# Two-layer graph network: the blocks of the adjacency matrix that are checked for symmetry are transposed by DMA instead of by TensorE

## The chip, the cores and the metric

The kernel runs on one core of a Trainium2 chip. A core has TensorE for matrix products (PE in the profile, its weight loads PEld), VectorE (DVE), ScalarE (ACT), GpSimd (POOL) and SyncE (SP), which here only issues DMAs. Each engine works through its own queue in order, and semaphores tie the queues together. The metric is the time of one execution on the device, in microseconds; lower is better. The kernel before takes 1238.69 us, the median of three runs from 1237.64 to 1240.6.

## What is computed

Sixteen graphs of 1024 nodes with 128 features go through two layers. The first is masked attention in which a node attends to its neighbours; the second is three GraphSAGE convolutions with batch normalisation over an adjacency that has been thinned row by row ("dilated"). Cut to what matters:

```python
# x: (16, 1024, 128); adj: (16, 1024, 1024) of 0 and 1, symmetric, with ones on the diagonal
h = maximum(layernorm(x), 0)
q, k, v = (relu(h @ W.T + b) for W, b in ((Wq, bq), (Wk, bk), (Wv, bv)))
att = softmax((q @ k.T) * adj - 9e15 * (1 - adj))
x = x + relu(att @ v @ Wo.T + bo)

h = maximum(layernorm(x), 0)
def step(carry, n):                      # over the rows n, in order
    row = carry[n]
    num = sum(row)
    sf = where(num > 10, (num + 1) // 2, 1)
    rm = row & (cumsum(row) % sf == 0) if num > 1 else 0
    carry[n] &= ~rm; carry[:, n] &= ~rm
adj_d = scan(step, adj > 0)
for Wr, Wx, b, g, be in three convolutions:
    out = (adj_d @ h / deg) @ Wr + h @ Wx + b
    h = bn(relu(out / norm(out)), g, be)
x = x + concatenate([h1, h2, h3]) @ Wl + bl
```

## The kernel before

The kernel has a fast path for inputs of this shape and a general one for all others. The fast path keeps checks of the input beside its work (`verdict`, line 449): zeros and ones only, diagonal full, adjacency symmetric, and some sizes. If a check fails, the general path runs afterwards. The check for symmetry is what the change touches.

**The attention loop.** One step per batch, 16 steps. A step has 2 x 8 scores: TensorE multiplies a block of 128 keys with 512 queries (line 697), ScalarE takes the exponential (line 699), VectorE multiplies it with the adjacency (line 700), and half a step later TensorE multiplies the result with the values (line 713). The step is cut into 48 ticks (`TICKS`), three to a score. `pace` (line 811) runs once a tick: it emits what was put off to this tick (`clock`), and then advances every generator of an agenda that has this tick in its list. The lists (`AT_PROJECT`, `AT_LOAD`, `AT_BOUND`, `AT_MIRRORS`, `AT_SORT`, `AT_GATHER`, `AT_NORMS`, `AT_STORE`, lines 735 to 750) are written out by hand. So the order of the instructions in each engine's queue is the order of the ticks, and no scheduler changes it. Most lists differ for even and odd steps. In step 0 the lists are squeezed into the second half of the step.

**The adjacency.** During step i the rows of batch i+1 are loaded (`load`, line 158): eight times a DMA of 512 KB by SyncE into one of three staging tiles `st`, then a pass of ScalarE that writes the bf16 tile `ab` and sums the rows, and a second pass that counts zeros (`AT_LOAD`: every third tick from tick 1, two ticks to a row block). `ab` has two buffers.

**The check for symmetry.** `mirrors` (line 214) has nine parts at the ticks of `AT_MIRRORS`: the first counts the diagonal (`count_loops`, line 208, which writes a throw-away tile `junkv`), the other eight are `mirror(b, k)` (line 180). For row block k TensorE transposes the k+1 blocks of the column up to the diagonal into a PSUM tile (line 186, 1 to 8 transposes, 36 a batch), and one tick later VectorE compares this tile with `ab`'s row, two bf16 at a time as int32, and sums what differs into `odd` (line 192). The PSUM tile comes from a pool of two (`bank`, line 152) that the other parts of the dilation use too.

**The rest of the dilation.** `bound` (line 221) decides step by step which nodes are "special"; its eight small products wait for `d_away` from VectorE. In odd steps `sort` and `gather` (lines 239 and 284) follow for two batches. `gather` has 13 parts: four that make `onehot`, one product, the rows' index with an indirect DMA of GpSimd (`rows`, line 301), a scan by VectorE (line 305), the codes (line 308), eight transposes by TensorE (line 312), two evictions (line 316), a product (line 320), and the codes' store. `AT_GATHER` has the ticks of these 13 parts, for the even batch within the step and the tick after it, for the odd batch in the next step. `solve` (line 330) then iterates over groups of four batches.

**Where the layers meet.** After step 15 there are 22 more ticks with the last values (line 882). What is left of the agenda then, parts of the last gather alone, goes with the last `solve` into a generator `last_of_dilation` (line 899). It is advanced beside the first convolution by `beside1` (line 1073), eight times a batch, so that `PIECES1` parts are spread evenly over `TICKS1` = 120 of its ticks.

The queues that matter: SyncE issues the adjacency loads, the loads of `x`, and later loads and stores, in program order; GpSimd issues the indirect DMAs, that is the gathers' rows and the scatter of each batch's result (line 540).

Of the kernel before, what the change touches and what calls it, by code (L numbers as in the profile page):

```python
# [8 lines left out]
BF = mybir.dt.bfloat16  # L9
H16 = mybir.dt.float16  # L10
I32 = mybir.dt.int32
AF = mybir.ActivationFunctionType
OP = mybir.AluOpType
AX = mybir.AxisListType

P = 128
B, N, D = 16, 1024, 128
NB = N // P
# [18 lines left out]
LAST = 12  # L37
# [18 lines left out]
class Clock:  # L56


    def __init__(self):
        self.now, self.queue = 0, []  # L60
# [20 lines left out]
class Dilation:  # L81
# [7 lines left out]
    def __init__(self, tc, adj, accT, ones, jp, identf, pool, psum, rows, rows_psum, clock):  # L89

        self.nc, self.adj = tc.nc, adj
        nc = self.nc
        self.accT, self.ones = accT, ones
        self.pick = {}
        self.pool, self.psum, self.rows, self.rows_psum, self.put_off = pool, psum, rows, rows_psum, clock.later
        own = self.pool

        def const(name, shape, dtype=F32):
            return own.tile(shape, dtype, name=name, bufs=1)

        self.identf = identf
        self.identb, self.identh = (const(f"d_id{i}", [P, P], t) for i, t in enumerate((BF, H16)))
        for t in (self.identb, self.identh):
            nc.vector.tensor_scalar(t, jp, 0.0, None, op0=OP.is_equal)
        self.up = const("d_up", [P, P], BF)
        nc.vector.tensor_scalar(self.up, jp, 0.0, None, op0=OP.is_gt)
        self.after = const("d_after", [P, P], BF)
        nc.vector.tensor_scalar(self.after, jp, 0.0, None, op0=OP.is_lt)
        nc.vector.scalar_tensor_tensor(self.after, self.identb, BIG, self.after, op0=OP.mult, op1=OP.add)
        self.onesb = const("d_ones", [P, P], BF)  # L110
        nc.vector.memset(self.onesb, 1.0)
        self.onesf = const("d_onesf", [P, P])
        nc.vector.memset(self.onesf, 1.0)
        self.half = const("d_half", [P, 1], BF)
        nc.vector.memset(self.half, 0.5)
        self.one_k = const("d_one_k", [P, 1])
        nc.vector.memset(self.one_k, -ONE_K)
        ii = const("d_ii", [P, S], I32)
        nc.gpsimd.iota(ii, pattern=[[1, S]], base=1, channel_multiplier=0)
        self.iota = const("d_iota", [P, S], H16)  # L120
        nc.vector.tensor_copy(self.iota, ii)
        mi = const("d_mi", [P, NB], I32)
        nc.gpsimd.iota(mi, pattern=[[P, NB]], base=0, channel_multiplier=1)
        self.node = const("d_node", [P, NB])
        nc.vector.tensor_copy(self.node, mi)
        self.node32 = mi
        self.node16 = const("d_node16", [P, NB], H16)
        nc.vector.tensor_copy(self.node16, mi)
        self.first = [const(f"d_first{i}", [P, NB, 2], BF) for i in range(2)]
        self.away = [const(f"d_away{i}", [P, 2, NB, 3], BF) for i in range(2)]  # L130
        self.limits = [const(f"d_limits{i}", [P, NB, 2]) for i in range(2)]
        self.neghalf = const("d_neghalf", [P, 1], BF)
        nc.vector.memset(self.neghalf, -0.5)
        for t in self.away + self.first:
            nc.vector.memset(t, 1.0)

        self.deg = const("d_deg", [P, B, NB])
        self.zeros = const("d_zeros", [P, B, NB])
        self.odd = const("d_odd", [P, B, NB])
        self.loops = const("d_loops", [P, B])  # L140
        self.sizes = const("d_sizes", [P, B, 2])
        self.used = const("d_used", [P, B])
        self.code = const("d_code", [P, B, S], H16)
        self.own = const("d_own", [P, B, P], BF)
        self.dcode = const("d_dcode", [P, B])
        self.moved = const("d_moved", [P, B])
        self.kept_deg = const("d_kdeg", [P, B])
        self.slot = const("slot", [P, B, NB], I32)
        self.A = {}
        self.tail = False  # L150

    def bank(self, shape, dtype, own=False):
# [5 lines left out]
    def load(self, b):  # L158
# [5 lines left out]
        for k in range(NB):  # L164
# [12 lines left out]
                nc.scalar.activation(junk, st, AF.Exp, scale=-ZERO_K, accum_out=zeros)  # L177
            yield

    def mirror(self, b, k):  # L180

        nc = self.nc
        ab, diag = self.A[b]
        pt = self.bank([P, NB, P], BF)
        for j in range(k + 1):
            nc.tensor.transpose(pt[:, j, :], ab[:, j, k * P:(k + 1) * P], self.identb)
        n = (k + 1) * P // 2

        def compare():

            junk = self.rows.tile([P, NB, P], BF, name="junkv", bufs=1)
            nc.vector.scalar_tensor_tensor(junk.rearrange("p a b -> p (a b)")[:, :n],
                                           pt.rearrange("p a b -> p (a b)").bitcast(I32)[:, :n], 1.0,
                                           ab[:, k, :].bitcast(I32)[:, :n], op0=OP.mult, op1=OP.not_equal,
                                           accum_out=self.odd[:, b, k:k + 1])

        self.put_off(1, compare)

    def prepare(self, b):

# [6 lines left out]

    def count_loops(self, b):
        nc = self.nc
        junk = self.rows.tile([P, NB, P], BF, name="junkv", bufs=1)  # L210
        nc.vector.scalar_tensor_tensor(junk, self.A[b][1], 1.0, self.identb[:, None, :].to_broadcast([P, NB, P]),
                                       op0=OP.mult, op1=OP.mult, accum_out=self.loops[:, b:b + 1])

# [299 lines left out]
def fast(ctx: ExitStack, tc: tile.TileContext, a, out, vp):  # L513
    nc = tc.nc
# [119 lines left out]
    late = ExitStack()  # L634
# [6 lines left out]
    with ExitStack() as s1:  # L641
        att = s1.enter_context(tc.tile_pool(name="att", bufs=2))
        aps = s1.enter_context(tc.tile_pool(name="aps", bufs=2, space=PSUM))
        dil = Dilation(tc, adj, accT, kept, jp, identf, dpool, dpsum,
                       rows.enter_context(tc.tile_pool(name="adj", bufs=2, side="right")), aps, clock)
# [79 lines left out]
        def store(b):  # L725
            for k in range(NB):
# [10 lines left out]
                      for m in ([1, 9, 14, 15, 16], [0, 1, 3, 5, 6])]  # L737
        AT_LOAD = every(1, 2 * NB, 3)
        AT_BOUND = [[0] + [first + 3 * (j // 2) + j % 2 for j in range(2 * NB)] for first in (9, 3)]
        AT_MIRRORS = ([11, 20, 23, 29, 33, 35, 39, 42, 44], [11, 13, 16, 19, 22, 25, 29, 33, 41])  # L740

        AT_SORT = [27, 29, 31, 32, 33, 35, 36]
        AT_GATHER = ([37, 38, 39, 41, 44, 45, 51, 55, 59, 60, 61, 65, 66],
                     [68, 69, 70, 71, 74, 75, 81, 85, 89, 90, 91, 93, 94])
        AT_NORMS = ([30, 57, 67, 68, 71], [42, 44, 58, 67, 70])
        AT_STORE = every(75, NB, 2)
# [2 lines left out]
        agenda = []  # L749
        gathering = {}  # L750

        def plan(gen, start, ticks):
            agenda.append((gen, [start + t for t in ticks]))

        def solve_pieces(b0, b1):
            return 9 * ITER + 3 + 13 * (b1 - b0)

        def plan_step(i):

            start, odd = i * TICKS, i % 2  # L760
            if i == 0:

                late = lambda ticks: [TICKS // 2 + t // 2 for t in ticks]
                plan(values0, start, [3, 6, 9, 12])
            else:
                late = lambda ticks: ticks
            plan(dil.bound(i), start, late(AT_BOUND[odd]))
            plan(dil.mirrors(i), start, late(AT_MIRRORS[odd]))
            if i + 1 < B:
                plan(project(i + 1), start, late(AT_PROJECT[odd]))  # L770
                plan(load_adj(i + 1), start, late(AT_LOAD))
            if odd:
                plan(dil.sort(i - 1), start, AT_SORT)
                for b, ticks in zip((i - 1, i), AT_GATHER):
                    gathering[b] = dil.gather(b)
                    plan(gathering[b], start, ticks)
            if i:
                last = i == B - 1
                plan(norms_of_x2(i - 1, att), start, LAST_NORMS if last else AT_NORMS[odd])
                plan(store(i - 1), start, LAST_STORE if last else AT_STORE)  # L780
            for b0, b1, t0, t1 in GROUPS:
                if t0 // TICKS == i:
                    n = solve_pieces(b0, b1)
                    plan(dil.solve(b0, b1), 0, [t0 + j * (t1 - t0) // n for j in range(n)])
# [3 lines left out]
        def load_adj(b):  # L788
            g = dil.load(b)
            next(g)  # L790
            AB_[b] = dil.A[b][0]
            yield
            yield from g
# [15 lines left out]
        tick = 0  # L809
# [75 lines left out]
        for t in range(22):  # L885
# [3 lines left out]
            b = t // 4 - 1  # L889
# [2 lines left out]
                    H[b] = enter(b)  # L892
                _advance(H[b][1])
        clock.flush()
        assert all(gen is gathering[B - 1] for gen, ticks in agenda if ticks)
        dil.tail = True
    load_x2(2)

    def last_of_dilation():

        yield from gathering[B - 1]
        yield from dil.solve(LAST, B)

    def last_stores():
# [158 lines left out]
    with tc.tile_pool(name="ps1", bufs=2, space=PSUM, reuse_waits="tile") as ps:  # L1063
# [3 lines left out]
        checks = dil.verdict(a["nodemask"], vp, recips)  # L1067
        _advance(checks)

        tick, TICKS1, PIECES1 = 0, 8 * (B - 1), 13 + solve_pieces(LAST, B)  # L1070
        entering = iter(())

        def beside1():
# [782 lines left out]
```

## Time and profile before

| | |
|---|---|
| median of three runs | 1238.69 us |
| the profiled execution | 1234.29 us |
| its span, first to last instruction | 1232.4 us |
| TensorE busy in the span | 1095.0 us (89%), 7775 products |
| VectorE, ScalarE, GpSimd busy | 881.5, 726.6, 573.6 us |
| mean granted TensorE clock | 0.96 |
| line 186, the transposes of adjacency blocks | 576 |
| line 192, their compares | 128 |
| adjacency loads (512 KB each), median to landing | 128, 3.7 us |
| row gathers, median to landing | 16, 4.9 us |

The attention loop takes up about the first 770 us, the first convolution runs to about 920, the other two and the output fill the rest. A line of the timeline or of a group names the line of the code, the engine, the operation and the tiles (written tile, arrow, read tiles), then shapes. In square brackets stands how long the engine had been idle, and what ended that wait. The engines' queues overlap the end of one instruction with the start of the next, so that durations in a row add up to more than the time they take; the distance of starts shows that.

The waits of SyncE's own queue are few and long in the attention loop: it has 8 adjacency loads and one load of `x` to issue in a step of some 46 us.

### The profile page before, as it was taken

To read this page: it belongs to the slowest core of one execution; us is meant where nothing else is said; L and a number is where in the kernel's file an instruction comes from. 1 tells how busy PE (TensorE), PEld (TensorE's weight loads), DVE (VectorE), ACT (ScalarE), POOL (GpSimd) and SP (SyncE) were. 2 spreads that over 40 slices of the span, in tenths; PEclk is the share of its full clock that TensorE was granted. 3 is DMA by queue.
4 is the path that set the end of the run, shared out by engine and by line. 5 is a ranking of instruction groups with operands and counts; after the bars stand their busy time and mean duration, and the time that the engine had idled before them with its cause. 6 is when DMAs were issued, how large, how long until landed. Compare 5 with 4: busy or idle time off the path is not lost. (4 is left out here: it accounts for less than half of the span.)

```text
span 1232.4 us, 22348 instructions
## 1 busy us (share of the span) xinstructions
PE 1095.0 (89%) x7775; PEld 820.4 (67%) x7775; DVE 881.5 (72%) x2630; ACT 726.6 (59%) x1570; POOL 573.6 (47%) x1082
## 2 busy tenths in 40 slices
PE   4899999999899899899899888588769979999894
PEld 2467677666576676566567656477658758988773
DVE  5767567579788578678778778589877876666642
ACT  5578788777677777678677652266554542333320
POOL 0330752651742742743644524769400004777686
PEclk9899999999999999999999999789889989999897
DMA  6544244344244344244334411415000013778564
GB/s 197 157 132 139 92 139 152 99 130 150 87 137 144 98 137 153 86 126 151 97 127 122 125 31 39 122 42 135 1 1 1 1 35 109 228 218 239 167 185 126
DMA packets 118147, 143.45 MB, mean 116 GB/s; under 512 B 9212, under 2 KB 94088, under 8 KB 118024
## 3 DMA queue, kind: packets, MB, share of 16 engines
q1 hardware_dynamic: 106120, 110.78, 30.3%
q0 software_dynamic: 11904, 31.15, 7.7%
q8 instruction: 63, 1.03, 0.4%
q14 instruction: 60, 0.49, 0.1%
HBM read 113.39 MB, written 28.51 MB: 115 GB/s over the span
## 5 line engine op out<-in xcount | busy, mean ns | idle before, releaser
L713 PEld LDWEIGHTS po<-vw,e 128*128 128x128 f32 x2048 | 273.1, 195 | 65.7 <-issue 65.3
L713 PE MATMUL po<-vw,e 128*128 128x129 f32 x2048 | 306.9, 284 | 0.0
L697 PE MATMUL ps<-qT,kT 128*128 128x512 f32 x512 | 272.0, 615 | 0.8 <-ACT e L699 0.8
L700 DVE TENSOR_TENSOR e<-e,ab 128x512 f32<-128x512 f32 x256 | 177.9, 696 | 110.4 <-ACT e L699 108.8
L699 ACT ACTIVATE e<-ps 128x512 f32<-128x512 f32 x256 | 153.0, 598 | 107.1 <-PE ps L697 84.4
L540 POOL DMA_INDIRECT x_d<-xt,slot x128 | 142.6, 1114 | 38.8 <-issue 34.9
L167 ACT ACTIVATE ab<-st,d_one_k 128x1024 bf16<-128x1024 f32 x128 | 146.9, 1148 | 0.3 <-DMA st<-in_adj_dram 0.3
L576 POOL TENSOR_SCALAR ln_t<-ln_st 128x8 f32<-128x8 f32 x31 | 8.0, 258 | 288.5 <-DVE ln_st L569 230.0
L177 ACT ACTIVATE junk<-st 128x1024 bf16<-128x1024 f32 x112 | 118.3, 1056 | 0.0
L540 POOL DMA_INDIRECT y_d<-y,nodes x88 | 86.2, 979 | 29.1 <-issue 28.6
L722 ACT ACTIVATE o<-po,recips 128x128 f32<-128x128 f32 x128 | 46.7, 367 | 72.1 <-DVE recips L720 72.0
L697 PEld LDWEIGHTS ps<-qT,kT 128*128 128x128 f32 x512 | 79.0, 194 | 7.6 <-issue 3.1
L1019 ACT ACTIVATE r<-pt 128x512 f32<-128x512 f32 x74 | 44.5, 601 | 58.7 <-PE pt L1007 58.7
L588 POOL TENSOR_SCALAR hn<-xt,ln 128x128 f32<-128x128 f32 x120 | 75.9, 644 | 1.6
L965 ACT ACTIVATE sq<-po 128x512 f32<-128x512 f32 x80 | 47.7, 596 | 47.1 <-PE po L956 44.1
L951 PE MATMUL po<-ws,r 128*128 128x128 f32 x512 | 74.8, 292 | 0.0
L305 DVE TENSOR_TENSOR_SCAN left<-rows 128x1024 f16<-128x1024 f32 x16 | 38.2, 2389 | 50.1 <-DMA rows<-in_adj_dram,row 50.1
L1016 DVE BATCH_NORM_STATS2 stats<-r 128x6 f32<-128x512 f32 x74 | 50.9, 689 | 29.4 <-ACT r L1019 28.9
L951 PEld LDWEIGHTS po<-ws,r 128*128 128x128 f32 x512 | 64.9, 199 | 8.6 <-issue 6.8
L968 DVE TENSOR_REDUCE nrm<-sq 128x4 f32<-128x512 f32 x80 | 53.9, 676 | 22.8 <-ACT sq L965 21.4
L1149 POOL COPY mark<-y 128x1 f32<-128x1 f32 x30 | 5.7, 191 | 135.7 <-DVE y L1024 132.8
L588 POOL TENSOR_SCALAR hn<-xt 128x128 f32<-128x128 f32 x112 | 55.9, 510 | 27.0 <-PE pt L598 26.2
(300 smaller groups left out, 2426.8 us busy)
## 6 DMA issues: line engine op xcount, KB each, us to landing
st<-in_adj_dram SPq DMA_DIRECT2D x128, 512.0 KB, 3.7
r<-y_d SPq DMA_DIRECT2D x22, 512.0 KB, 5.2
xt<-x_d SPq DMA_DIRECT2D x16, 524.0 KB, 3.8
xt<-in_x_dram SPq DMA_DIRECT2D x16, 512.0 KB, 4.2
x<-x_d SPq DMA_DIRECT2D x16, 512.0 KB, 4.4
out_dram<-r SPq DMA_DIRECT2D x11, 512.0 KB, 3.4
x_d<-xt,slot POOLq DMA_INDIRECT x128, 2.8
y_d<-y,nodes POOLq DMA_INDIRECT x88, 3.5
```

The source lines that it names most:

```text
L167: nc.scalar.activation(ab[:, k, :], st, AF.Exp, bias=self.one_k, scale=ONE_K, accum_out=self.deg[:, b, k:k + 1])
L177: nc.scalar.activation(junk, st, AF.Exp, scale=-ZERO_K, accum_out=zeros)
L540: d = nc.gpsimd.indirect_dma_start(out=dst, out_offset=bass.IndirectOffsetOnAxis(ap=slots, axis=0), in_=src, in_offset=None)
L588: engine.tensor_scalar(hn[:, k, :], xt[:, k, :D], minus[:, k // 2, k % 2, None], rstd[:, k // 2, k % 2, None], op0=OP.add, op1=OP.mult)
L697: nc.tensor.matmul(p, K[b][:, k * P:(k + 1) * P], Q[b][:, c], start=True, stop=True)
L699: later(1, lambda: nc.scalar.activation(e, p, AF.Exp))
L700: later(2, lambda: nc.vector.tensor_mul(e, e, AB_[b][:, k, c]))
L713: nc.tensor.matmul(po[:, q % 2, :], E[k][:, i * P:(i + 1) * P], V[b][:, k, :], start=(k == 0), stop=(k == NB - 1))
L951: nc.tensor.matmul(po[:, i, :], hT[:, c:c + P], wxk, start=(i == 3), stop=False)
L965: later(1, lambda: nc.scalar.activation(sq, halves[g], AF.Square))
L968: nc.vector.tensor_reduce(n[:, 0, 4 * g:4 * g + 4], sq, axis=AX.X, op=OP.add)
L1016: nc.vector.bn_stats(stats[:, 2 * b + g, :], d)
```

## The change

The transposes of the check go from TensorE to DMAs, which SyncE issues. A new generator `turn_rows` takes, for k from 0 to 7, the first (k+1) x 128 columns of `ab`'s row block k and writes its blocks, each transposed, into a tile of its own in SBUF (`mirrored0` to `mirrored7`, one buffer each). `mirror` then is the compare alone: it takes the next of these tiles, compares it with the column of blocks in `ab` that it should equal, and writes the result of the compare over the tile. Before, the column was transposed and compared with the row.

The generator is advanced at the ticks of a new list, `AT_TURN`, the same in all steps: 12 to 15 and 20 to 23 (in step 0 squeezed like the others). At these ticks its DMAs fall between the adjacency loads in SyncE's queue: two each behind the loads that are counted 1 and 2 from 0, four behind load 3. `count_loops` writes into `mirrored7` now. The compares are emitted at the tick at which they were put off to before (the tick of `AT_MIRRORS` and one more).

Two smaller edits go with it. In even steps' gathers the transposes of the codes and their two evictions come two ticks later (61, 62, 63). And in `last_of_dilation` empty parts are put between the parts of the last gather: six behind the part that issues the rows' DMA, five behind the codes. Eleven parts of this gather are left there, and `PIECES1` now counts them as they are, with the empty ones: 11 + 11 + the solver's 118, where before it was 13 + 118.

```diff
+    def turn_rows(self, b):
+        ab = self.A[b][0]
+        for k in range(NB):
+            pt = self.rows.tile([P, k + 1, P], BF, name=f"mirrored{k}", bufs=1)
+            self.nc.sync.dma_start(pt, ab[:, k, :(k + 1) * P], transpose=True)
+            self.mirrored.append(pt)
+            yield
+
     def mirror(self, b, k):
-        nc = self.nc
-        ab, diag = self.A[b]
-        pt = self.bank([P, NB, P], BF)
-        for j in range(k + 1):
-            nc.tensor.transpose(pt[:, j, :], ab[:, j, k * P:(k + 1) * P], self.identb)
-        n = (k + 1) * P // 2
-        def compare():
-            junk = self.rows.tile([P, NB, P], BF, name="junkv", bufs=1)
-            nc.vector.scalar_tensor_tensor(junk.rearrange("p a b -> p (a b)")[:, :n],
-                                           pt.rearrange("p a b -> p (a b)").bitcast(I32)[:, :n], 1.0,
-                                           ab[:, k, :].bitcast(I32)[:, :n], op0=OP.mult, op1=OP.not_equal,
-                                           accum_out=self.odd[:, b, k:k + 1])
-        self.put_off(1, compare)
+        pt = self.mirrored.pop(0)
+        self.nc.vector.scalar_tensor_tensor(pt.bitcast(I32), pt.bitcast(I32), 1.0,
+                                            self.A[b][0][:, :k + 1, k * P:(k + 1) * P].bitcast(I32), op0=OP.mult,
+                                            op1=OP.not_equal, accum_out=self.odd[:, b, k:k + 1])
...
-        junk = self.rows.tile([P, NB, P], BF, name="junkv", bufs=1)
+        junk = self.rows.tile([P, NB, P], BF, name="mirrored7", bufs=1)
...
+        AT_TURN = [12, 13, 14, 15, 20, 21, 22, 23]
...
-        AT_GATHER = ([37, 38, 39, 41, 44, 45, 51, 55, 59, 60, 61, 65, 66],
+        AT_GATHER = ([37, 38, 39, 41, 44, 45, 51, 55, 61, 62, 63, 65, 66],
...
-            plan(dil.mirrors(i), start, late(AT_MIRRORS[odd]))
+            plan(dil.turn_rows(i), start, late(AT_TURN))
+            plan(dil.mirrors(i), start, late([t + (j > 0) for j, t in enumerate(AT_MIRRORS[odd])]))
...
-        assert all(gen is gathering[B - 1] for gen, ticks in agenda if ticks)
+        (gather_left,) = (len(ticks) for gen, ticks in agenda if ticks)
...
+    GATHER_IDLE = {5: 6, 7: 5}
     def last_of_dilation():
-        yield from gathering[B - 1]
+        for part in range(13 - gather_left, 13):
+            next(gathering[B - 1])
+            for _ in range(1 + GATHER_IDLE.get(part, 0)):
+                yield
         yield from dil.solve(LAST, B)
...
-        tick, TICKS1, PIECES1 = 0, 8 * (B - 1), 13 + solve_pieces(LAST, B)
+        tick, TICKS1, PIECES1 = 0, 8 * (B - 1), gather_left + sum(GATHER_IDLE.values()) + solve_pieces(LAST, B)
```

More of the change, by code (lines that the diff above doesn't have):

```diff
@@ L149, in __init__ @@
         self.A = {}
+        self.mirrored = []
         self.tail = False
```

## The prediction

> **What bounds the kernel now.** I read first the busy time of the engines in each step of the attention loop (a step is one of the 16 batches; I cut the windows where VectorE forms `du`, the first instruction of a step), because all removed work lies there. The columns are the window, its length, then busy time and count of TensorE, its weight loads, VectorE, ScalarE, GpSimd, then clock, DMA share and rate.
>
> ```profile
> 69.90:113.10 43.20, 43.20 (x303) 31.06 (x303) 27.66 (x97) 34.52 (x65) 10.67 (x23) 1.00 0.41 112
> ...
> 248.70:295.10 46.40, 45.82 (x343) 32.89 (x342) 38.29 (x142) 35.78 (x70) 24.45 (x45) 1.00 0.42 128
> 295.10:345.10 50.00, 42.23 (x318) 29.43 (x318) 39.80 (x137) 34.11 (x68) 23.45 (x45) 1.00 0.38 122
> ...
> 69.90:770.00 700.10, 653.78 (x4673) 462.23 (x4673) 526.12 (x1788) 502.25 (x975) 327.50 (x631) 0.99 0.38 116
> ```
>
> The reader is to see that TensorE is busy for 653.8 of 700.1 us over steps 1 to 15, VectorE for 526 and ScalarE for 502. In odd steps TensorE hardly pauses (0.0 us in step 1, 0.6 in step 5); in even ones it does (7.8 us in step 6). Second, the timeline of TensorE around one row of adjacency blocks: start, duration, instruction, count.
>
> ```profile
> 339.58 0.61 PE L713 MATMUL po<-vw,e 128*128 128x129 f32 x4
> 340.03 0.61 PE L186 MATMUL pd<-d_id,ab 128*128 128x128 bf16 x8
> 340.47 1.08 PE L697 MATMUL ps<-qT,kT 128*128 128x512 f32 x2
> ```
>
> The durations overlap; the starts don't. Eight transposes hold TensorE from 340.03 to 340.47, 0.055 us each. Third, the waits of steps 1 to 14 (us in total, times, longest), and the timeline where the last gather's tail meets the next layer:
>
> ```profile
> PE pd L233 <- DVE d_away L236: 7.4, 11, 1.4
> ...
> PE pd L312 <- DVE codes L308: 7.0, 7, 1.8
> ```
> ```profile
> 794.01 1.07 POOL L301 DMA_INDIRECT rows<-in_adj_dram,row  x1 [0.16 <-issue]
> ...
> 799.12 3.80 DVE L305 TENSOR_TENSOR_SCAN left<-rows 128x1024 f16<-128x1024 f32 x1 [8.70 <-DMA rows<-in_adj_dram,row]
> 802.95 1.28 DVE L308 SCALAR_TENSOR_TENSOR codes<-rows,left 128x1024 f16<-128x1024 f32 x1
> ...
> 804.29 1.04 PE L312 MATMUL pb<-d_id,codes 128*128 128x128 f16 x8 [12.05 <-DVE codes L308]
> ```
>
> TensorE stands still for 12.05 us in one place, because VectorE stands 8.70 us behind rows that had not landed. Last, what SyncE does, since the new transfers are issued there, and what VectorE's compare costs:
>
> ```profile
> SPq L166 <- ACT junk L177: 355.4, 80, 8.1
> ```
> ```profile
> q1 hardware_dynamic: 106120, 110.78, 30.3%
> ...
> st<-in_adj_dram SPq DMA_DIRECT2D x128, 512.0 KB, 3.7
> ```
> ```profile
> L700 DVE TENSOR_TENSOR e<-e,ab 128x512 f32<-128x512 f32 x256 | 177.9, 696 | 110.4 <-ACT e L699 108.8
> ...
> L192 DVE SCALAR_TENSOR_TENSOR junkv<-pd,ab 128x512 bf16<-128x512 int32 x16 | 11.0, 688 | 5.9 <-PE pd L186 5.9
> ```
>
> SyncE mostly waits for ScalarE to free a staging tile, 4.4 us each time; the DMA engines carry 30% from its queue.
>
> **What the Trainium skill says.** "VectorE: DVE Perf Modes", section "The three transpose paths", gives a 128x128 bf16 transpose 390 ns on TensorE and 1309 ns through the DMA crossbar. For TensorE the trace says 219 ns for one and 55 ns in a row, and the latter is what counts here. "Advanced Engine Details and Errata", section "X-Bar Transpose (TRN2)", calls such DMAs as fast as plain ones, 350 to 400 GB/s. The two disagree by an order of magnitude once transposes follow each other: the blocks of a step are 36 x 32 KB = 1.18 MB, an estimate of 3 us by the second page and, added up, of 36 x 1.309 = 47 us by the first. No run so far shows a DMA transpose. "DMA: Bandwidth & Descriptors", section "Rules for kernel authors", says that DMAs of all queues share the same 16 engines, and that a transpose beside ordinary DMAs needs no ordering. The trace shows those engines 38% busy in steps 1 to 15.
>
> **TensorE loses 576 transposes.** 36 a step x 0.055 = 1.98 us a step, 31.7 us in all. What of it counts depends on whether TensorE sets the pace there. In the seven odd steps from 1 to 13 its idle time is together 3.4 us: I count 95%, 7 x 1.98 x 0.95 = 13.2 us. The seven even steps from 2 to 14 have 38.1 us of idle time, waits for VectorE's bursts, for GpSimd's `hn` and for solver results; a transpose ahead of such a wait only makes the wait longer. Most transposes of an even step lie in its second half (30 of 36 from tick 29 on) and most of those waits in its first: I count 70%, 9.7 us. Step 15 (4.8 us idle) half, 1.0; step 0, where TensorE is busy 25.2 of the 30 us from 40 to 70, 60%, 1.2. Sum 25.1 us; with every wait growing it is some 14, with none 31.7.
>
> **VectorE's compare reads the block from SBUF.** The nearest row is L700, 512 f32 elements from SBUF in 696 ns, against 688 for 512 int32 from PSUM; the eight compares keep their lengths. Cost nothing, between -2 and +2 us of VectorE's time, hidden as long as VectorE is 75% busy. VectorE's 14.8 us of waiting for those transposes goes too, and nothing hung on it. If a block were late, VectorE would stand at the compare, behind it the products for the next values and so TensorE; but the last block is issued at about tick 12 and compared at tick 42 or later, some 28 us.
>
> **SyncE issues 128 transposes, eight a step, between the adjacency loads.** Counting a batch's loads from 0, they stand behind load 1 (two), load 2 (two) and load 3 (four), and loads 4 to 7 of the next batch stand behind them. In step 5 load 3 can go when ScalarE frees its tile at about 254.0; the four transposes behind it hold 26 of the 36 blocks. The eighth waits for the loop count that VectorE ends at 261.2 (both write one tile); load 4 had been due at 259.7, so it goes some 1.5 us late. It is needed by ScalarE at 272.3 and takes 3.7 to land: it may leave at 268.6. So these 26 blocks have 14.6 us, or 0.56 us each, before anything stands still. Lower bound: a DMA issue of 0.33 us each, 2.6 us a step. Upper: 1.31 us a block. I take one to two us an instruction, which hides: cost 0. The engines' load, 1.18 MB to about 5.4 MB a step, hides too.
>
> **Later transposes of even codes.** TensorE waits 7.0 us in seven steps at L312; two ticks (1.9 us) later the codes are there. But in the crowded steps TensorE next waits for `d_away`, 7.4 us in all, behind the same VectorE burst, and it would reach that wait earlier. I count 2.5 us of the 7.0, and 1.0 for the eighth such gather, after step 15, which waits 4.34 us. Together 3.5; bounds 0 and 8.
>
> **Idle ticks behind the last gather.** 11 parts of it are left and 11 idle ones are put in, 140 parts with the solver's 118 in 120 ticks, 1.17 a tick. A tick is about 0.83 us there (8 to a batch of some 6.6 us). The rows are issued at 794.0 by GpSimd's queue order, which stays, and land at 799.1. Seven parts are six ticks, so VectorE comes to the scan after about 5 us, some 795, and still waits 4; the 5.1 us of scan and code remain, but TensorE has five more parts of other work before it needs them. I count a stall of 5.5 instead of 12.05: 6.5 us gained, between 3 and 10. What is late next is the solver, begun some nine ticks later at a pace 7% denser; its end is at the same tick.
>
> **Sum.** 25.1 + 3.5 + 6.5 = 35.1 us. The profiled execution took 1234.3 us (span 1232.4), so it becomes 1199; the runs' median of 1238.7 is 0.36% above it, and becomes 1203.6. I forecast 1204.
>
> **Rivals.** (a) Another engine takes over: TensorE's lead turns into waits for ScalarE (36 of 46 us in odd steps, exp and the adjacency passes in one queue) and VectorE (38 of 46). Speaks for it: the even steps already show it. Against: 8 to 10 us of room in each odd step. Only a quarter of the 31.7 us is kept, 8, with 1 and 3 of the rest: 12 us, 1226. (b) The DMA transposes take the place of the bound. If each block holds the queue for 1.31 us, a step needs 47.1 + 9 other issues x 0.33 = 50.1 us of SyncE against the mean step of 46.7, and loads 4 to 7 come behind 34 us of transposes: at least 15 x 3.4 = 51 us more, less 10 from the gather edits: 1280 or above. It begins to cost above 0.56 us a block and decides at about 0.65, where 26 blocks are the 2 us a step late that TensorE gains. For it: the first page's figure. Against: the second page's[...]. (c) Gains and losses cancel, as when blocks take about that critical time: 1238.
>
> **How the numbers follow.** Forecast 0.62, its own range 1188 to 1216. Rival (a) 0.22, from 1216 to 1234. Rival (c) 0.03. Rival (b) 0.13. A range from 1186 to 1231 leaves out (b), (c) and the edges of the first two, about 0.2. About 0.2% (2.5 us) is what a measurement can tell from no change. Faster 0.84, the same 0.03, slower 0.13.
>
> **What would show it.** Right: no L186 on TensorE; odd steps of about 44 us instead of 46, with TensorE still busy almost throughout; SyncE's adjacency loads landing ahead of ScalarE's need; no wait at L312's successor in even steps; a wait near 800 of about 5 us instead of 12. Wrong: ScalarE waiting for `st` in steps 1 to 14, VectorE waiting for a transposed block, odd steps with several us of TensorE idle time, or a scan at 799 with TensorE stopped as long as before.

## The result and the profile after

The changed kernel takes 1232.44 us (median of 9 runs, 1227.11 to 1235.57) beside 1240.08 us for the kernel before (9 runs, 1237.42 to 1241.73). The ratio is 0.9932, with a 95% interval from 0.9912 to 0.9953: some 8 us faster, where 35 were forecast. The time is just outside the range (1186 to 1231).

The profiled executions happen to be equally long (1234.43 and 1234.29 us): that of the kernel before is shorter than all nine of its timed runs, 5.8 us under their median, and that of the changed kernel is among its long ones, 2.0 us above. So the profile is read for what moved, and the medians for what it was worth. First the engines' busy time by step in the changed kernel: the window, its length, then busy time and count of TensorE, its weight loads, VectorE, ScalarE, GpSimd, then granted clock, DMA share and rate. The first three rows are steps 1, 5 and 6, the last is steps 1 to 14.

```profile
68.48:110.35 41.87, 41.87 (x269) 29.00 (x268) 27.34 (x100) 34.82 (x65) 10.97 (x23) 1.00 0.56 144
248.76:294.19 45.43, 43.33 (x307) 30.79 (x306) 38.03 (x141) 36.10 (x70) 25.82 (x45) 1.00 0.58 141
294.19:350.13 55.94, 44.74 (x282) 31.11 (x282) 39.90 (x137) 33.64 (x66) 23.46 (x45) 0.85 0.52 137
...
68.48:729.67 661.19, 597.43 (x3881) 416.14 (x3880) 487.39 (x1654) 485.83 (x944) 327.03 (x608) 0.96 0.55 147
```

Steps 1 to 14 of the kernel before, the same view:

```profile
69.89:727.33 657.44, 615.90 (x4383) 434.70 (x4383) 490.66 (x1653) 488.17 (x944) 313.80 (x608) 0.99 0.40 122
```

Fourteen steps have lost 4383 - 3881 = 502 recorded products, 27.6 us at 0.055 us each, but TensorE's busy time fell by 18.5 us only, and the stretch is no shorter in these two executions. TensorE's idle time in it (length less busy time) went from 41.5 to 63.8 us. Odd steps became shorter, as forecast: step 1 from 43.2 to 41.9, the seven from 1 to 13 from 317.2 to 308.7. Even steps became longer: step 6 from 50.0 to 55.9, the seven from 2 to 14 from 340.2 to 352.5. In step 6 the clock column says 0.85: the granted clock was at half for 30% of the step. Over steps 1 to 14 the trace's clock records show 58.0 us at half clock, against 17.1 before, all of it in even steps.

The seven even steps account for most of what was lost. TensorE's busy time in them fell from 302.1 to 298.6 us, 3.5 us where 13.9 us of transposes had gone; the missing 10.4 us stand beside 40.9 us more at half clock. Its idle time in them grew from 38.1 to 53.9 us. In the seven odd steps the busy time fell by 14.9 us, about what had gone, and the idle time grew from 3.4 to 9.9.

What TensorE waits for in steps 1 to 14 (us in all, times, longest):

```profile
PE pd L231 <- DVE d_away L234: 23.6, 16, 6.1
PE pm L674 <- ACT qT L675: 11.6, 6, 3.5
...
PE pm L596 <- POOL hn L586: 8.9, 7, 1.8
```

The wait for the codes (7.0 us before) is gone; the one for `d_away` is 23.6 instead of 7.4, and those for `qT` and `hn` grew from 5.1 to 11.6 and from 7.2 to 8.9. The longest is in step 6. Its timeline, put together from SyncE, GpSimd, VectorE and TensorE (start, duration, instruction, idle time before it and what ended that):

```profile
289.86 2.41 SPq L186 DMA_TRANSPOSE mirrored<-ab  x2
291.14 1.01 POOL L299 DMA_INDIRECT rows<-in_adj_dram,row  x1 [5.22 <-DVE theta L371]
...
298.92 2.29 DVE L303 TENSOR_TENSOR_SCAN left<-rows 128x1024 f16<-128x1024 f32 x1 [2.56 <-DMA rows<-in_adj_dram,row]
...
306.97 0.15 DVE L234 TENSOR_TENSOR d_away<-pd,d_limits 128x2 bf16<-128x2 f32 x1
...
307.17 0.16 PE L231 MATMUL pd<-d_away,ab 128*128 128x2 bf16 x1 [6.14 <-DVE d_away L234]
...
310.31 2.05 PE L695 MATMUL ps<-qT,kT 128*128 128x512 f32 x2
```

The reader is to see a chain: VectorE's scan of the rows began 7.8 us after their DMA was issued (5.1 us in this step before, without a wait), VectorE waited 2.56 us for them, then had the scan, the codes and a solver round in its queue ahead of the tiny comparison that TensorE needs, and TensorE stood for 6.14 us. Two products of 512 columns that take 1.08 us elsewhere then took 2.05.

Where the layers meet, in the same view:

```profile
795.61 1.07 POOL L299 DMA_INDIRECT rows<-in_adj_dram,row  x1 [0.16 <-DVE ob L1004]
...
800.97 4.55 DVE L303 TENSOR_TENSOR_SCAN left<-rows 128x1024 f16<-128x1024 f32 x1 [4.96 <-DMA rows<-in_adj_dram,row]
...
806.88 1.03 PE L310 MATMUL pb<-d_id,codes 128*128 128x128 f16 x8 [4.20 <-DVE codes L306]
```

TensorE stops for 4.20 us there instead of 12.05. Last, SyncE's issues in step 5 (timeline), and from the page the DMA queues (packets, MB, share of the 16 engines) and issues (count, size, median us to landing):

```profile
250.21 2.49 SPq L186 DMA_TRANSPOSE mirrored<-ab  x2
...
255.00 8.05 SPq L186 DMA_TRANSPOSE mirrored<-ab  x4
```

```profile
q1 hardware_dynamic: 183944, 129.67, 39.9%
...
st<-in_adj_dram SPq DMA_DIRECT2D x128, 512.0 KB, 4.5
...
mirrored<-ab SPq DMA_TRANSPOSE x128, 4.1
```

Two transposing DMAs hold SyncE for 2.49 us, 1.24 each (the 8.05 us for four hold a wait for VectorE as well). The trace tells the landing of 16 of the 128; their median is 4.1 us. No compare of VectorE waited for one, and the compares kept their lengths (686 ns for 512 int32 from SBUF, 688 from PSUM before). The queue's share rose from 30.3% to 39.9%, and adjacency loads take 4.5 us to land (16 landings told) instead of 3.7 (32 told), but behind the very first load ScalarE's waits for them come to 0.9 us.

### The profile page after: what moved, and what is told of

It is laid out like the page before. It is cut to its first block, busy times and chain, and to the rows that moved or that the text cites. A ratio compares the mean times of both kernels' runs of the same rounds, so it can differ in the third digit from the quotient of the medians.

```text
span 1232.5 us, 21344 instructions
## 1 busy us (share of the span) xinstructions
PE 1070.2 (87%) x7199; PEld 795.4 (65%) x7199; DVE 879.0 (71%) x2630; ACT 724.6 (59%) x1570; POOL 587.5 (48%) x1082
## 2 busy tenths in 40 slices
DMA packets 195968, 162.28 MB, mean 132 GB/s; under 512 B 87036, under 2 KB 171912, under 8 KB 195848
## 3 DMA queue, kind: packets, MB, share of 16 engines
q1 hardware_dynamic: 183944, 129.67, 39.9%
## 5 line engine op out<-in xcount | busy, mean ns | idle before, releaser
L711 PEld LDWEIGHTS po<-vw,e 128*128 128x128 f32 x2048 | 278.2, 198 | 78.8 <-issue 75.3
L538 POOL DMA_INDIRECT x_d<-xt,slot x128 | 147.2, 1150 | 40.6 <-issue 36.9
L975 DVE TENSOR_REDUCE nrm<-sq 128x4 f32<-128x512 f32 x80 | 53.9, 676 | 25.4 <-ACT sq L972 24.0
```

Source lines behind the costliest of these rows:

```text
L538: d = nc.gpsimd.indirect_dma_start(out=dst, out_offset=bass.IndirectOffsetOnAxis(ap=slots, axis=0), in_=src, in_offset=None)
L711: nc.tensor.matmul(po[:, q % 2, :], E[k][:, i * P:(i + 1) * P], V[b][:, k, :], start=(k == 0), stop=(k == NB - 1))
L975: nc.vector.tensor_reduce(n[:, 0, 4 * g:4 * g + 4], sq, axis=AX.X, op=OP.add)
```

## The experiments

All are timed against the kernel before on the same chip. Chips differ: before takes 1279 us on two of them, 1236 on two, 1240 in the first comparison. (Each of those four was used on one occasion, so that chip and occasion can't be told apart.) Ratios of one chip are compared first. The microseconds in the expectations of the first four runs are those of a chip where before takes 1240.

| run | this, us | before, us | ratio and 95% interval |
|---|---|---|---|
| DMA transposes alone | 1263.53 | 1278.82 | 0.9883 [0.9853, 0.9914] |
| no transposes | 1257.51 | 1278.82 | 0.9845 [0.9817, 0.9873] |
| DMAs issued later | 1262.36 | 1278.82 | 0.9892 [0.9858, 0.9927] |
| no later codes | 1254.22 | 1278.82 | 0.9819 [0.9786, 0.9852] |
| later codes alone | 1284.44 | 1278.87 | 1.0044 [1.0024, 1.0064] |
| idle ticks alone | 1274.31 | 1278.87 | 0.9961 [0.9942, 0.9980] |
| no transposes, no later codes | 1256.83 | 1278.87 | 0.9801 [0.9765, 0.9838] |
| changed kernel (chip of the three rows above) | 1258.41 | 1278.87 | 0.9844 [0.9803, 0.9886] |
| filler products | 1230.94 | 1236.21 | 0.9954 [0.9936, 0.9971] |
| comparisons begun later | 1224.98 | 1236.21 | 0.9915 [0.9888, 0.9943] |
| the same, no later codes | 1219.93 | 1236.21 | 0.9881 [0.9847, 0.9915] |
| changed kernel (chip of the next rows) | 1227.46 | 1235.62 | 0.9916 [0.9889, 0.9944] |
| odd steps put back | 1236.46 | 1235.62 | 1.0003 [0.9981, 1.0025] |
| even steps put back | 1226.70 | 1235.62 | 0.9896 [0.9865, 0.9927] |
| no later codes, again | 1226.78 | 1235.62 | 0.9906 [0.9871, 0.9940] |

**The parts apart.** The DMA transposes alone: the changed kernel with the codes at their old ticks and no idle ticks.

```diff
-    GATHER_IDLE = {5: 6, 7: 5}
+    GATHER_IDLE = {}
-... 51, 55, 61, 62, 63, 65, 66]
+... 51, 55, 59, 60, 61, 65, 66]
```

> The DMA transposes alone; the code transposes of even batches stay at ticks 59 to 61, and no idle parts behind the last gather. Theory A (the transposing DMAs are in flight when the even batch's rows are gathered, so the rows land late, VectorE stands in order behind them, TensorE pauses and its clock is halved): even steps as long as in the changed kernel, last pause 12 us as before, 1234 to 1238. Rival B (in even steps other engines set the pace, so nothing that TensorE loses there counts): the same, about 1234. Rival C (the later code transposes move TensorE's stop to a worse place): faster than the changed kernel, 1226 to 1230.

The gain is 15 us of 1279. Next, the later codes and the idle ticks, each put alone into the kernel before:

> The kernel before with the code transposes of even batches two ticks later, nothing else. The prediction: 2 to 4 us faster than before (ratio 0.997). Rival C (TensorE skips the stop at the codes only to stop longer at d_away, whose VectorE instruction stands behind the same burst): no gain or slower, ratio 1.000 to 1.006, with the waits at d_away grown by as much as those at the codes shrink.

> The kernel before with the idle parts behind the last gather, nothing else. The prediction: 6.5 us faster (ratio 0.995), the pause of 12 us near 800 down to about 5. If the next stage only waits elsewhere: ratio 0.998 to 1.000.

The idle ticks gain 5.0 us (0.0039 x 1279; 6.5 were counted, within the interval). The later codes cost 5.6 us instead of gaining. TensorE's waits of steps 1 to 14 show what was exchanged, first in the run with idle ticks alone, where the codes are at their old place, then in that with the later codes:

```profile
PE pd L312 <- DVE codes L308: 7.9, 7, 1.8
PE pd L233 <- DVE d_away L236: 7.6, 12, 1.4
```

```profile
PE pd L233 <- DVE d_away L236: 16.7, 16, 3.5
```

Seven short stops for the codes are gone, and 16 for `d_away` stand where there were 12: 9 us more for 8 us less, and the longest grew from 1.8 to 3.5. That is 1 us of the 5.6. Where the rest lies isn't shown: the first of these executions was 4.7 us above its median, the second 2.0 under its own.

**Do the DMAs cost?** Two runs leave the transposing DMAs out and let the compare read the block's own column twice, so they leave out the check of symmetry; the second also has the codes at their old ticks. A third issues all eight DMAs behind load 3 and moves the compares of odd steps to suit, to keep the DMAs clear of the even steps' row gathers.

```diff
-            self.nc.sync.dma_start(pt, ab[:, k, :(k + 1) * P], transpose=True)
```

> The changed kernel without the transposing DMAs: the compares stay, with the same shapes, and compare each column of blocks with itself, so the check for symmetry is left out. Nothing collides with the gathers. Theory A: even steps lose their late rows and most of the new half-clock time, 1216 to 1221. Rival B: within 3 us of the changed kernel, 1229 to 1234, with half-clock time as long as there. Rival C: also within 3 us.

> As the changed kernel, without the transposing DMAs (each compare reads its column twice, the check for symmetry is left out) and without the two ticks' shift. If the collision with the gathers is what costs: some 8 us faster than the kernel with the transposes and without the shift (which had ratio 0.982 on its chip), 0.975. If the freed time of TensorE goes into waits for other engines whatever the DMAs do: 0.979 to 0.984.

```diff
+        AT_TURN_LATER = [20] * 4 + [21] * 4
-... [11, 13, 16, 19, 22, 25, 29, 33, 41])
+... [11, 21, 22, 23, 24, 25, 29, 33, 41])
```

> The changed kernel with all eight transposing DMAs of a batch behind adjacency load 3 (in SyncE's queue some 6 us later), away from the even gathers; the first compares of odd steps come later in the order, since the tile has to be there. Theory A: rows land about 4.9 us after their issue in all even steps, 1219 to 1224. Rival B: 1229 to 1234. Rival C: 1229 to 1234.

> The changed kernel with the code transposes of even batches back at ticks 59 to 61. Theory A and rival B: 1231 to 1236, TensorE stops at the codes instead of at d_away. Rival C: 1222 to 1227.

> The changed kernel, unaltered, beside the three others on one chip. If the shift costs nothing (theory A, rival B): the same ratio as without the shift, about 0.982 on a chip like the last, 0.985 or lower. If the shift costs (rival C): 0.988 to 0.994.

Without any DMA the changed kernel runs at 0.9845 on one chip; with them at 0.9844 on another of the same speed. With the codes at their old ticks the pair is 0.9801 without and 0.9819 with DMAs. So by the medians the DMAs cost 0 to 2 us; the intervals would allow some 6 to 8, since each pair is of two chips. Issuing them later doesn't help (0.9892). Single row gathers land late in the changed kernel (7.8 us from issue to scan in step 6), but they do so without the DMAs too: in the run with neither DMAs nor later codes, 8.1 us in step 6 and 7.1 in step 14. There VectorE waits 7.6 us in all for the first gathers of the seven even steps (3.0 in the other run without DMAs), against 6.2 in the changed kernel and 0.5 before. So the transposing DMAs aren't needed for that. Nor is it where the forecast gain went: even transposes that are free gain only 1274.31 - 1256.83 = 17.5 us over the idle ticks alone on one chip, and 31.7 were taken from TensorE.

**The half clock.** The Trainium skill's page "TensorE: Matmul & The Clock Gate", section "Part 1: The HAM clock gate", says that the array falls to half rate after an idle window of about 3.4 us, and its section "Why this matters for your kernels" would have no gaps above some 3 us. The traces agree in kind: the half-clock stretches of the changed kernel's attention loop are all 3.4, 6.8 or 10.2 us long and begin some microseconds behind pauses. But such pauses were often shorter than either figure: the longest in the 9 us ahead of a stretch was 1.46 us in one case (at 224.5), and 1.0 us in the kernel before (at 226.1). To test the price, 40 products without use fill the place where TensorE stood for `d_away`:

```diff
+            if k == 1 and b and b % 2 == 0:
+                for _ in range(40):
+                    nc.tensor.matmul(pf[:, 2:], self.identb, self.identb, start=True, stop=True)
```

> The changed kernel; in the seven even steps from 2 to 14, TensorE gets 40 multiplications of the identity by itself (128x128 bf16, 0.055 us each, 2.2 us a step, 15.4 us in all, results unused) just ahead of the second product for the next values, where it stood 1.7 to 7.1 us for d_away in five of those steps. Nothing else is altered. Theory (a pause there costs twice: itself, and the stretch of half clock that follows): the half-clock time of the attention loop falls from 58 us by 10 to 25 us, and the kernel takes no longer, or up to 6 us less, than the changed kernel (1258 beside a before of 1279), though it does 15 us of work more. Rival (the clock does not matter, what bounds is VectorE's arrival): half-clock time as before and the kernel 3 to 8 us slower, from the two steps where TensorE didn't stand there.

The windows of step 6 and of steps 1 to 14 of that run:

```profile
294.38:347.56 53.18, 44.70 (x322) 31.87 (x322) 39.95 (x137) 33.54 (x66) 24.07 (x45) 0.94 0.53 141
...
68.77:726.60 657.83, 606.44 (x4161) 427.53 (x4160) 488.95 (x1655) 485.87 (x944) 325.42 (x608) 0.97 0.55 147
```

Half-clock time fell to 41.0 us and step 6 to 53.2 us, although it does more. But the ratio, 0.9954, is not better than the changed kernel's 0.9932 and 0.9916 on other chips: both readings of the expectation were half wrong. Filling this pause took the half-clock time down as the first had it, and bought nothing. Whether the fillers' own 15.4 us of work ate a gain isn't shown.

**Where does TensorE's time count?** Two runs put the 36 transposes back on TensorE, with nobody reading them, in the odd or in the even steps of the changed kernel. (They stand a tick later than they did before, beside the compare, and take their PSUM tile from the same pool of two.)

```diff
+        if b % 2:
+            again = self.bank([P, NB, P], BF)
+            for j in range(k + 1):
+                self.nc.tensor.transpose(again[:, j, :], self.A[b][0][:, j, k * P:(k + 1) * P], self.identb)
```

> The changed kernel unaltered, beside the next three on one chip, so that they are compared with it there. Expected: a ratio to before between 0.984 and 0.994, as in the two comparisons so far.

> The changed kernel, in whose odd steps (1 to 15) the 36 transposes of a step run on TensorE again, a tick's work ahead of the compare, with nobody reading them: 288 x 0.055 = 15.8 us of TensorE's time. The DMA transposes and the compare stay. This prices TensorE's time alone. The prediction counted 95% of it in steps 1 to 13 and half in step 15: 14.2 us. Theory (TensorE sets the pace in odd steps): 9 to 15 us slower than the changed kernel beside it, odd steps longer by 8 to 13 us together. Rival (the odd steps became shorter by another way, the compare or the PSUM tiles that it held): less than 5 us slower.

> The same in the even steps from 2 to 14: 252 x 0.055 = 13.9 us of TensorE's time, of which the prediction counted 70%, 9.7 us. Theory (in even steps the freed time goes into waits for other engines and into the half clock behind them): less than 4 us slower than the changed kernel beside it, or faster, with less half-clock time. Rival (the freed time is kept there, and something else that the change brought made even steps longer): 8 to 12 us slower.

On one chip, 15.8 us of TensorE's time in odd steps cost 1236.46 - 1227.46 = 9.0 us (10.8 by the ratios); 13.9 us in even steps cost -0.8 us, nothing that can be told. Both differences are uncertain by some 4 us. Steps 5, 6, and 1 to 14, first of the changed kernel there, then with the odd steps put back:

```profile
247.83:293.25 45.42, 43.33 (x307) 30.79 (x306) 38.37 (x141) 36.07 (x70) 25.79 (x45) 1.00 0.57 141
293.25:348.61 55.36, 43.42 (x282) 30.03 (x282) 39.76 (x138) 33.56 (x66) 22.95 (x45) 0.88 0.55 139
...
68.44:727.78 659.34, 593.72 (x3881) 413.28 (x3880) 488.50 (x1653) 485.18 (x944) 322.57 (x608) 0.96 0.55 147
```

```profile
250.46:297.52 47.06, 45.77 (x343) 32.98 (x342) 38.36 (x142) 36.49 (x70) 24.90 (x45) 1.00 0.59 149
297.52:346.88 49.36, 41.09 (x282) 28.40 (x282) 39.81 (x138) 33.44 (x66) 23.99 (x45) 0.97 0.53 136
...
69.07:731.31 662.24, 605.25 (x4133) 425.36 (x4132) 489.11 (x1654) 487.57 (x944) 323.75 (x608) 0.97 0.55 146
```

This is the telling pair. Work put into odd steps makes them longer (step 5 by 1.6 us, the seven together from 308.0 to 321.5) and makes the even steps, which were left as they are, shorter (step 6 by 6.0 us, the seven from 351.3 to 340.8). A good part of what an odd step gains is lost in the even step behind it. The execution profiled here for the changed kernel was its longest of six, so 10.5 us overstates the return: by the medians 9.0 us of 15.8 are kept. TensorE's busy time in the even steps, which have the same work in both, is 5.1 us less with the odd steps put back (295.0 and 289.9, with 51.2 and 34.1 us at half clock), its idle time 5.5 us less.

How a lead is lost can be seen in step 6, first in the changed kernel, then with the odd steps put back:

```profile
290.19 1.00 POOL L299 DMA_INDIRECT rows<-in_adj_dram,row  x1 [5.24 <-DVE theta L371]
...
299.03 2.29 DVE L303 TENSOR_TENSOR_SCAN left<-rows 128x1024 f16<-128x1024 f32 x1 [3.61 <-DMA rows<-in_adj_dram,row]
```

```profile
294.12 1.00 POOL L303 DMA_INDIRECT rows<-in_adj_dram,row  x1 [7.51 <-DVE theta L375]
...
299.61 2.28 DVE L307 TENSOR_TENSOR_SCAN left<-rows 128x1024 f16<-128x1024 f32 x1
```

The changed kernel enters step 6 4.3 us earlier (293.25 and 297.52) and issues the rows' DMA 3.9 us earlier, but the rows take 8.8 us instead of 5.5 to the scan, which so begins only 0.6 us earlier; the first `d_away` comes 0.6 us earlier too (307.08 and 307.64). The transposing DMAs are in both runs. What holds the rows up wasn't found.

The even steps put back, steps 1 to 14:

```profile
68.44:726.13 657.69, 606.16 (x4133) 426.77 (x4132) 487.57 (x1655) 487.23 (x946) 324.68 (x608) 0.97 0.56 148
```

12.4 us more of busy TensorE than in the changed kernel beside it, and 1.6 us less in length, in an execution that was 4.3 us shorter as a whole.

**The comparison out of the way.** `bound` begins four ticks later in even steps, with the codes late as in the change, and then at their old ticks:

```diff
-        AT_BOUND = [... for first in (9, 3)]
+        AT_BOUND = [... for first in (13, 3)]
```

> The changed kernel, with the products and comparisons for the next values begun four ticks later in even steps (tick 13 instead of 9), so that VectorE's scan (tick 3) and code (tick 7) of the even gather have more time ahead of the first comparison at tick 14. Theory (TensorE's freed time is lost at this comparison, behind VectorE's burst): the waits for d_away fall from 24 us to under 12, half-clock time to under 45 us, and the kernel is 4 to 10 us faster than the changed one. Rival (the even steps are bound by VectorE or ScalarE altogether): the wait only turns up elsewhere (hn, qT, the transposes of codes), pauses sum to as much, time within 2 us of the changed kernel.

> As the run with the comparisons begun at tick 13, and the transposes of even codes back at their old ticks (59, 60, 61). Theory (the later transposes cost time since they leave TensorE to stop at d_away instead): with the comparisons out of the way the shift matters less, so this is within 3 us of the run with the comparisons begun later, and both are 4 to 10 us faster than the changed kernel. Rival (the shift costs by itself): it is 4 us or more faster than that run, near 1250 beside a before of 1279.

> The changed kernel with the transposes of even codes at their old ticks (59, 60, 61). On the first chip where it ran it was 4 us faster than the changed kernel, and the later ticks cost the kernel before 5.6 us. Theory (they take a short stop for the codes and give a longer one for d_away): 3 to 7 us faster than the changed kernel beside it. Rival (a gain of 3.5 us by the later ticks, as predicted): 3 to 4 us slower.

TensorE's waits with the comparisons begun later:

```profile
PE pm L596 <- POOL hn L586: 12.8, 12, 2.9
PE pm L674 <- ACT qT L675: 11.2, 8, 3.0
PE pd L231 <- DVE d_away L234: 9.8, 18, 2.1
...
PE pd L318 <- ACT turned L314: 5.4, 6, 1.2
```

The wait for `d_away` fell from 23.6 to 9.8 and half-clock time to 30.7 us, as the theory had it, but the ratio moved little (0.9915; 4 to 10 us had been expected): waits for `hn` and `turned` and for the codes (4.6) took a part of it. With the codes at their old ticks as well it is 0.9881, 1219.93 us, the fastest measured beside a before of 1236. It beats the kernel before by 16 us; that it beats the changed kernel (1227.46 us on another chip whose before takes 1235.62) is likely, but the intervals overlap. It isn't a run of short waits: TensorE waits 16.2 us for the codes there, so which wait it saves isn't shown. On one chip the codes' old ticks by themselves changed nothing that could be told (0.9906 against 0.9916), where 3 to 7 us had been expected.

## Why the prediction missed

It had the sign and some of the places right, and the sum was too large by a factor of four. The step that failed is the price of TensorE's time in even steps. Step by step:

- **SyncE and the DMAs at cost 0: right.** One to two us an instruction was taken, 1.24 measured; the waits named as signs of trouble (ScalarE for `st`, VectorE for a block) didn't come. Removing the DMAs altogether gains 0 to 2 us by the medians. The rival in which they become the bound fell. VectorE's compare at cost 0 was right too (686 and 688 ns).
- **Idle ticks, 6.5 us: right.** Alone they gain 5.0, with an interval from 2.6 to 7.4; the stop is 4.20 us where 5.5 was forecast.
- **Odd steps, 95% of 13.9, 13.2 us (and 1.0 for step 15): the shortening is there, smaller.** The seven odd steps became 8.5 us shorter in the profile. Putting the work back, in step 15 too, costs 9.0 us where 14.2 had been counted, which is at the edge of what the intervals allow. The 1.2 us of step 0 weren't tried.
- **Even steps, 70% of 13.9, 9.7 us: wrong.** Putting it back costs -0.8 us. This is the step that failed most. The prediction subtracted the stops from the room but let the rest of the step be TensorE's; the runs show the freed time going into stops that end with other engines' chains (idle time 38.1 to 53.9 us) and into busy time that grew beside the half clock (10.4 us). Its ground, that most of the stops lie in the first half of a step and most transposes behind them, holds only in part: in the trace of before 23.5 of the 38.1 us lie in the second half of the steps, 14.8 of them behind the place of tick 29, among the transposes. (By `AT_MIRRORS`, 33 and not 30 of a step's 36 come from tick 29 on.)
- **Later codes, +3.5 us: wrong in sign or at least in size.** Alone they cost 5.6 us (1.0044, interval above 1); taken out of the changed kernel they show nothing that can be told on one chip. The prediction named the mechanism, that TensorE "would reach that wait earlier" for `d_away`, and gave it 4.5 of the 7.0 us; in the traces that wait took more than the whole.
- **Not in the sum at all: the steps' coupling and the clock.** The prediction added savings step by step. The two steps of a pair are one unit here: over steps 1 to 14 a pair takes 93.9 us before (657.4 / 7), 94.5 in the changed kernel, 94.2 in its second profile, 94.6 with the odd and 94.0 with the even steps put back. These are single executions, up to 5.8 us off their medians, so good to some 0.8 us a pair, but 3.96 us of TensorE's work a pair had been removed. Half-clock time, which a price list of full-speed instructions leaves out, more than tripled to 58 us at the same time.

What came about is the mechanism of rival (a), TensorE's lead turned into waits for other engines, with a gain of some 8 us where the rival had 12, and with the half clock that it did not name. Against it the prediction held "8 to 10 us of room in each odd step" for ScalarE and VectorE, busy time against length. That room was no proof: no engine is full in the even steps (VectorE 39.9 of 55.9 us in step 6), and still they don't get shorter; in step 6 rows, scan, codes, solver and comparison follow one upon another.

On the one chip, 9.0 for the odd steps, -0.8 for the even ones and 5.0 for the idle ticks (measured on another) give 13.2 us, beside 8.2 measured (1235.62 - 1227.46). The 5 us between them is as large as the experiments' uncertainty; the later codes and the DMAs may have a share in it. Two things stay open. On the chips where before takes 1279 us the transposes are worth twice as much (17.5 us when they are left out): the seven odd steps take 339 us there with the transposes on TensorE (in the runs with later codes and with idle ticks alone), against 317, and some 318 with the whole change. Most of those 22 us can be placed, from the run with idle ticks alone: TensorE's idle time in the odd steps is 17.5 us instead of 3.4, with four stops of some 3 us for `kT` from ScalarE that the kernel before doesn't have on the other chip, and 13.7 us are at half clock instead of none. What starts those stops wasn't found. And how much of the even steps' length is the half clock, and how much the chain of other engines, isn't separated: filling one pause lowered the one without shortening the time.

## What to carry to other kernels

A busy share of 94% doesn't say that an engine sets the pace: take the loop's real period (here two steps, since solver and gathers go over two), and ask of each stop inside it which chain ends it and whether that chain starts from work that you remove. A cheap test before a large rewrite is to leave the work out without replacing it: here that gave 17.5 us of 31.7 without a single new DMA. The reverse test, by stage, tells where: put work of the size that was saved back on the engine, and where it costs nothing, its removal gained nothing. And where a small instruction with a waiting reader stands behind a burst in an engine's queue, moving the reader's earlier stop away can lengthen the later one by as much (here 9 us for 8). Starting those readers later cut this wait from 23.6 to 9.8 us, but others grew, and the gain in time was too small to be told.

## What the runs showed of the hardware

- A DMA that transposes one to eight 128x128 bf16 blocks from SBUF to SBUF holds SyncE's queue for about 1.24 us (the median of 128), and nearly the same for all sizes: the medians are 1.12 us for one block and 1.23 for eight. In steps 5 and 6 two of them with 3 blocks together took 2.41 us, two with 7 blocks 2.49 and 2.61. The prediction had two estimates from the Trainium skill for a step's 36 blocks, 3 us ("Advanced Engine Details and Errata", section "X-Bar Transpose (TRN2)") and 47 us ("VectorE: DVE Perf Modes", section "The three transpose paths"). Neither is SyncE's price, some 10 us a step (8 x 1.24) beside other work. For the DMA engines an estimate lies between the two: the queue's share rose by 9.6% of 1232 us, 118 us in 16 steps, as if all 16 engines were busy for 7.4 us more a step.
- The transposes multiply the small packets: under 512 B the changed kernel has 87036 instead of 9212, while the adjacency loads slow down only a little (3.7 to 4.5 us in the first comparison, 4.0 in the second profile of the changed kernel).
- TensorE's half clock comes in stretches of 3.4 us or multiples of it here, and grew faster than the pauses did: in steps 1 to 14 it went from 17.1 to 58.0 us while pauses above 1.5 us went from 6 with 15.1 us to 14 with 41.2, and TensorE's idle time from 41.5 to 63.8.
- The same kernel before takes 1236 to 1240 us on some chips (or occasions) and 1279 us on others, and a change's ratio differs with it: 0.9844 on one of the latter, 0.9932 and 0.9916 on the former.
